# A build-time list scheduler reckons TensorE steps a tenth longer and adds a fixed wait to each step of the other compute engines

## Chip, cores and metric

One core of a Trainium2 chip runs the whole program in one launch. The metric is device microseconds of one execution, as the median of several. One further execution was taken with the hardware profiler; all durations and waits below come from it.

## What is computed

A conditioned block on x of 4 x 1024 tokens by 512 channels, all in float32: a normalised, modulated Mamba-like scan with a gated residual, then a normalised, modulated mixture of 8 experts (two per token) with another gated residual.

```python
mod = (_silu(c) @ wmod).reshape(4, 6, 1, -1)          # sa, ca, ga, sb, cb, gb
h = _layernorm(x) * (1 + ca) + sa
x = x + ga * attn(h)
h = _layernorm(x) * (1 + cb) + sb
x = x + gb * ffn(h)
...
# attn: a causal depthwise convolution of 4 taps gives u; then
x_dbl = u_bld @ xproj_w.T                              # 128 + 16 + 16 columns: dt, Bm, Cm
delta = softplus(dt @ dtproj_w.T + dtproj_b)
dA, dBu = exp(delta[..., None] * A), delta[..., None] * Bm[:, :, None, :] * u_bld[..., None]
h = dA * h + dBu                                       # over 1024 steps, 512 channels x 16 states
y = einsum('bdn,bn->bd', h, c) + u_bld * D_skip
...
# ffn: top 2 of 8 experts by tanh(x @ Wg1.T) @ Wg2.T, softmax over the two
up = einsum('td,ehd->teh', xt, Wup) + bup              # 256 hidden per expert
down = einsum('teh,eoh->teo', silu(up), Wdown) + bdown
out = einsum('te,teo->to', scores, down)
```

## The kernel before

**Tiling and stages.** The tokens are cut into nine blocks along the sequence: 512 tokens each for the first three batches (two blocks a batch), and 512, 384 and 128 for the last. Each block passes three parts. The *front* (`front`, with `conv`, `pre` and `post`) normalises, turns to channels-on-partitions, convolves, projects and makes delta and delta times u. The *recurrence* runs over 64 units a block, one for each of 16 states and 4 chunks of 128 channels. The *back* (`back`, `router`, `scatter`) normalises again, routes, and scatters rows to their experts in DRAM; then `tiles` and `expert` run 128-row tiles of one expert each, 86 in all, and `combine` gathers each token's two rows. The last block of 128 tokens goes through all eight experts in `dense` without a scatter. A branch at the end (`rest`) holds tiles for token counts that overflow; it is not entered with these inputs.

**One unit of the recurrence** goes round four engines: dB, the product of duT and a column of B, on ScalarE (L878, two instructions of 128x256 a unit in a block of 512) or as one on GpSimd (L885); its turning by TensorE into a PSUM bank pb (L919, ring of 2); da, an exponential on ScalarE (L904, ring of 4); the scan h on VectorE (L937, ring of 2 pairs); the product hc with C on GpSimd (L955, ring of 5); the sum over the states into acc on TensorE (L994). The rows of C are spread by a DMA from SyncE's queue (cq, L854, ring of 4), which waits for a ring place that hc gives back. GpSimd also copies the last column of h into `state` for the next block (L963).

**One expert tile**: SyncE loads its rows and its expert's weights (L1368, L1370: 256 KB and 1 MB; a weight ring of 4, and a fifth buffer once the fronts are done); TensorE turns the rows (px, L1395), a copy takes them out (xT, L337 on ScalarE or L339 on VectorE), TensorE multiplies (pe, L1408), VectorE adds the bias (L1419), ScalarE takes a tanh (th, L1426), VectorE multiplies (hid, L1428), TensorE multiplies again (po, L1436), VectorE scales (L1446), and SyncE stores the rows (L1449).

**What sets the order.** The tile framework is put in manual mode, so each engine's instructions stand in the order in which Python emits them. That order is made by the class `Order` while the program is built. Every part above is a generator (a thread) that yields *steps*: an engine or a choice of engines, a cost, and events to wait for. `run` repeatedly takes the step that could begin first by its own clock, and, among those of the same engine that could begin within `TOGETHER` = 0.15 us of it, the one with the smallest due time; it then lets the thread emit the instructions and sets the engine's `free` time to the step's end. What depends on it may start `HANDOFF` later (0.30, 0.17, 0.22, 0.12 us for TensorE, VectorE, ScalarE, GpSimd). Due times stand on a fixed scale of 150 us a block of 512. Costs come from small formulas; for instance

```python
def t_mm(n, times=1):
    return times * 2 * max(0.112, 0.00084 * n)
...
def t_act(n, times=1):
    return times * (0.19 + 0.00083 * n)
```

with 0.11 us for a 128x128 turn, 0.09 + 0.00104 n for VectorE, 0.09 + 0.00215 n for a scan, and 0.05 + 0.0024 n for GpSimd. Steps by `either` may go to VectorE or ScalarE (normalisation L343/L345, copies L337/L339), steps by `both` to VectorE or GpSimd (delta L772, du L775), the D-skip product to any of the three (L780/L782/L784), and dB to ScalarE or GpSimd. `begins` chooses: earliest start plus cost plus handoff, and `OTHER` = 1.0 us is added to every engine but ScalarE. Nothing of this runs on the chip: there, each engine takes its instructions in the fixed order and waits on semaphores.

Of the kernel before, what the change touches and what calls it, by code (L numbers as in the profile page):

```python
# [97 lines left out]

PE, DVE, ACT, POOL, SP = range(5)
HANDOFF = (0.30, 0.17, 0.22, 0.12, 0.0)  # L100
TOGETHER = 0.15
OTHER = 1.0
TRANSFER, KB_PER_US, KB_ALONE = 4.0, 290.0, 150.0
# [76 lines left out]
class Order:  # L180
# [19 lines left out]
    def begins(self, th):  # L200
# [8 lines left out]
        if isinstance(eng, int):  # L209
            return max(r, self.free[eng]), eng, cost  # L210
        return min(
            ((max(r, self.free[e]), e, c) for e, c in eng), key=lambda s: s[0] + s[2] + HANDOFF[s[1]] + (0.0 if s[1] == ACT else OTHER)
        )

    def run(self):
        while self.threads:
            can = [(b, th) for th in self.threads if (b := self.begins(th)) is not None]
            if not can:
                raise RuntimeError("no thread can go on: " + str([th[0].__name__ for th in self.threads]))
            t0, eng, _ = min(can, key=lambda c: c[0][0])[0]  # L220
            (t, _, cost), th = min(
                (c for c in can if c[0][1] == eng and c[0][0] <= t0 + TOGETHER), key=lambda c: c[1][3]
            )
            self.eng, kb = eng, th[1][4]
            self.start = t
            self.free[eng] = t + cost
            self.fin = t + cost + HANDOFF[eng]
            if kb:
                self.moved[eng] = max(self.moved[eng], t + cost) + kb / KB_PER_US
                self.fin = max(self.moved[eng], t + cost + kb / KB_ALONE) + TRANSFER  # L230
            th[2] = self.fin
            th[3] += th[4]
            self.advance(th)
# [1487 lines left out]
```

## Time and profile before

| what | value |
|---|---|
| median of 3 runs (lowest to highest) | 1475.49 us (1470.91 to 1481.48) |
| the profiled execution's own time | 1469.49 us |
| its span, first to last instruction | 1467.8 us |
| mean granted TensorE clock in it | 0.924 |
| instructions in it | 24446 |
| scans (L937), first and last start | 64.9 and about 1354.6 us |

The profiled execution is 6.0 us below the median and 1.4 us below the lowest of the three runs. In the tables below a row of groups reads: line, engine, operation, output and inputs, size, count, then busy us, mean ns of one, idle time of the engine just before them and what ended it. A matmul's mean includes its way through the array, so four in a row take less than four means. Stretches of the trace are named by blocks: stage k is the time in which the scans of block k run; it begins with that block's first scan (stage 1 at 185 us, 2 at 325, 3 at 475, 4 at 647, 5 at 812, 6 at 976, 7 at 1134, 8 at 1281), and what follows the last scan, from 1355 us on, is the tail.

### The profile page before, as it was taken

To read this page: it belongs to the slowest core of one execution; us is meant where nothing else is said; L and a number is where in the kernel's file an instruction comes from. 1 tells how busy PE (TensorE), PEld (TensorE's weight loads), DVE (VectorE), ACT (ScalarE), POOL (GpSimd) and SP (SyncE) were. 2 spreads that over 40 slices of the span, in tenths; PEclk is the share of its full clock that TensorE was granted. 3 is DMA by queue.
4 is the path that set the end of the run, shared out by engine and by line. 5 is a ranking of instruction groups with operands and counts; after the bars stand their busy time and mean duration, and the time that the engine had idled before them with its cause. 6 is when DMAs were issued, how large, how long until landed. Compare 5 with 4: busy or idle time off the path is not lost. (4 is left out here: it accounts for less than half of the span.)

```text
span 1467.8 us, 24446 instructions
## 1 busy us (share of the span) xinstructions
PE 1239.5 (84%) x7716; PEld 930.3 (63%) x7716; DVE 1153.6 (79%) x1870; ACT 1065.0 (73%) x2127; POOL 1029.7 (70%) x1216
## 2 busy tenths in 40 slices
PE   5588687878789889998889989989899898898686
PEld 2456555665478657775567767777687666764454
DVE  4679989899988778898887988988889889557233
ACT  2789997799689585999687686888689867456110
POOL 1478986798588466788788856888889868557202
PEclk8799998899689998999799998999899999998698
DMA  4377754757499997653688978678999976985897
GB/s 175 112 180 147 147 146 106 190 166 163 132 269 299 263 255 217 202 158 89 200 260 297 330 215 225 209 249 262 243 305 268 281 206 231 327 241 141 306 337 215
DMA packets 141933, 321.63 MB, mean 219 GB/s; under 512 B 14899, under 2 KB 43475, under 8 KB 128998
## 3 DMA queue, kind: packets, MB, share of 16 engines
q1 hardware_dynamic: 111344, 254.35, 56.4%
q0 software_dynamic: 13888, 32.58, 10.4%
q10 hardware_dynamic: 16566, 33.08, 8.7%
q8 instruction: 63, 1.03, 0.3%
q14 instruction: 72, 0.59, 0.1%
HBM read 245.95 MB, written 82.40 MB: 224 GB/s over the span
## 5 line engine op out<-in xcount | busy, mean ns | idle before, releaser
L955 POOL TENSOR_TENSOR hc<-h,cq 128x512 f32<-128x512 f32 (+2 forms) x576 | 689.1, 1283 | 191.8 <-DVE h L937 114.8
L904 ACT ACTIVATE da<-delta,a_neg 128x512 f32<-128x512 f32 (+2 forms) x576 | 380.2, 668 | 115.4 <-DVE h L937 102.4
L919 PE MATMUL pb<-ident,dB 128*128 128x128 f32 x2048 | 350.0, 294 | 81.8 <-DVE h L937 70.2
L878 ACT ACTIVATE dB<-duT,bT 128x256 f32<-128x256 f32 x856 | 381.6, 498 | 32.4 <-PE pb L919 24.5
L994 PE MATMUL acc<-ident,hc 128*128 128x128 f32 x2048 | 344.5, 292 | 64.2 <-POOL hc L955 60.8
L919 PEld LDWEIGHTS pb<-ident,dB 128*128 128x128 f32 x2048 | 252.0, 150 | 179.7 <-DVE h L937 83.0
L937 DVE TENSOR_TENSOR_SCAN h<-da,state,pb 128x512 f32<-128x512 f32 (+2 forms) x320 | 329.4, 1053 | 37.7 <-PE pb L919 15.1
L994 PEld LDWEIGHTS acc<-ident,hc 128*128 128x128 f32 x2048 | 252.6, 149 | 143.1 <-POOL hc L955 102.2
L937 DVE TENSOR_TENSOR_SCAN h<-da,pb 128x512 f32<-128x512 f32 x256 | 304.8, 1208 | 48.4 <-PE pb L919 22.5
L1408 PEld LDWEIGHTS pe<-xT,w 128*128 128x128 f32 x1376 | 172.8, 195 | 31.0 <-issue 20.5
L1408 PE MATMUL pe<-xT,w 128*128 128x128 f32 x1376 | 185.9, 280 | 4.5 <-ACT xT L337 3.9
L1436 PE MATMUL po<-w,hid 128*128 128x512 f32 x344 | 179.1, 610 | 8.2 <-DVE hid L1428 7.4
L1485 POOL DMA_INDIRECT xc<-xs,idx x56 | 90.3, 1612 | 53.2 <-DMA xc<-xs,idx 25.2
L885 POOL TENSOR_TENSOR dB<-duT,bT 128x512 f32<-128x512 f32 (+1 forms) x88 | 88.6, 1016 | 27.0 <-PE pb L919 18.5
L1446 DVE SCALAR_TENSOR_TENSOR xs<-po,xs,gbh 128x512 f32<-128x512 f32 x86 | 63.7, 740 | 38.0 <-PE po L1436 37.0
L1323 POOL DMA_INDIRECT xs<-h,idx x62 | 63.8, 1029 | 27.6 <-POOL idx L1322 12.6
L1426 ACT ACTIVATE th<-pe 128x256 f32<-128x256 f32 x86 | 32.3, 376 | 60.6 <-DVE pe L1419 60.5
L1436 PEld LDWEIGHTS po<-w,hid 128*128 128x128 f32 x344 | 54.1, 194 | 25.3 <-issue 10.6
L337 ACT COPY xT<-px 128x512 f32<-128x512 f32 x78 | 44.9, 578 | 28.2 <-PE px L1395 28.1
L1419 DVE TENSOR_TENSOR pe<-pe,w 128x256 f32<-128x256 f32 x86 | 36.2, 421 | 36.2 <-PE pe L1408 33.9
L963 POOL COPY state<-h 128x2 f32<-128x2 f32 x160 | 59.2, 370 | 0.1
L1395 PE MATMUL px<-ident,xs 128*128 128x128 f32 x344 | 53.6, 280 | 1.6 <-ACT hT L343 0.8
(200 smaller groups left out, 1536.5 us busy)
## 6 DMA issues: line engine op xcount, KB each, us to landing
w<-w_all SPq DMA_DIRECT2D x86, 1025.0 KB
cq<-scr SPq DMA_DIRECT2D x224, 256.0 KB
xs<-xs SPq DMA_DIRECT2D x86, 256.5 KB
xs<-xs SPq DMA_DIRECT2D x86, 256.0 KB
xs<-xc ACTq DMA_DIRECT2D x16, 1026.0 KB
we<-w_all SPq DMA_DIRECT2D x8, 1025.0 KB
xf<-in_x SPq DMA_DIRECT2D x32, 256.0 KB
xr<-in_x SPq DMA_DIRECT2D x14, 512.0 KB
```

Of the source, the lines that this page charges most:

```text
L878: nc.scalar.activation(dB[u // 2].t[:, t, :], duT_sb[blk][half].t[:, t, :], AF.Identity, scale=bT_sb[blk].t[:, t, n : n + 1],)
L885: engine().tensor_tensor(dB[u // 2].t[:, t0:t1, :], duT_sb[blk][half].t[:, t0:t1, :], bT_sb[blk].t[:, t0:t1, n].unsqueeze(2).to_broadcast( ...
L904: nc.scalar.activation(da[u].t[:, :ln], delta_sb[blk][half].t[:, i, :ln], AF.Exp, scale=a_neg[:, dc, n : n + 1])
L919: nc.tensor.transpose(pbs[u][:, t * P : (t + 1) * P], dB[u // 2].t[:, t, i * P : (i + 1) * P], ident)
L937: nc.vector.tensor_tensor_scan(hs[u // 2].t[:, i, :ln], da[u].t[:, :ln], pbs.pop(u)[:, :ln], 0.0 if t0 == 0 else state[:, n, dc : dc + 1], ...
L955: nc.gpsimd.tensor_tensor(hcs[u].t[:, :ln], hs[u // 2].t[:, i, :ln], cq[u // 2].t[:, :ln], ALU.mult)
L994: nc.tensor.matmul(acc[blk, dc][:, t * P : (t + 1) * P], lhsT=src.t[:, t * P : (t + 1) * P], rhs=ident, is_transpose=True, start=False, st ...
L1323: i = nc.gpsimd.indirect_dma_start(out=xs_d[g], out_offset=bass.IndirectOffsetOnAxis(ap=idx[:, k, t : t + 1], axis=0), in_=h2[k].t, in_off ...
L1408: nc.tensor.matmul(pu[:, hc * P : (hc + 1) * P], lhsT=up[:, kc, hc * P : (hc + 1) * P], rhs=xT.t[:, kc, :], start=(kc == 0), stop=(kc == D ...
L1436: nc.tensor.matmul(po, lhsT=hid.t[:, hc * P : (hc + 1) * P], rhs=w.t[:, W_DN + hc * D : W_DN + (hc + 1) * D], start=(hc == 0), stop=(hc == ...
L1446: nc.vector.scalar_tensor_tensor(xs.t[:, :D], po, xs.t[:, D:], gbh[b].t, ALU.mult, ALU.mult)
L1485: nc.gpsimd.indirect_dma_start(out=a, out_offset=None, in_=xs_d[g], in_offset=bass.IndirectOffsetOnAxis(ap=idx_sb[blk][:, choice, t : t + ...
```

## The change

Two tuples are added, and in `run` a step's cost is multiplied (by 1.1 for TensorE) and raised (by 0.06 us for VectorE, ScalarE and GpSimd) before it is entered. Steps of 0.03 us or less (waits for a ring, with no instruction) keep their cost. The cost by which `begins` chooses an engine stays as it was. No instruction is added or removed by hand, and no buffer, ring or due time changes; what changes is the order of emission and, where an engine is chosen, the choice.

```diff
 HANDOFF = (0.30, 0.17, 0.22, 0.12, 0.0)
+PACE = (1.1, 1.0, 1.0, 1.0, 1.0)
+WAIT = (0.0, 0.06, 0.06, 0.06, 0.0)
 TOGETHER = 0.15
...
             self.eng, kb = eng, th[1][4]
+            if cost > 0.03:
+                cost = cost * PACE[eng] + WAIT[eng]
             self.start = t
             self.free[eng] = t + cost
             self.fin = t + cost + HANDOFF[eng]
```

The engines stand in the order TensorE, VectorE, ScalarE, GpSimd, SyncE.

## Prediction, made before the changed kernel was run

> **What bounds the kernel now.** I read the busy totals and the TensorE clock first, then a table by stage, then the waits of the stages in which scans and expert tiles mix, then the chain that ended last.
>
> ```profile
> PE 1239.5 (84%) x7716; PEld 930.3 (63%) x7716; DVE 1153.6 (79%) x1870; ACT 1065.0 (73%) x2127; POOL 1029.7 (70%) x1216
> PEclk8799998899689998999799998999899999998698
> ```
>
> No engine is full: the kernel is four queues in fixed orders that wait for each other. By stage (span, then busy us and count of PE, PEld, DVE, ACT, POOL, then the clock, the DMA share and GB/s):
>
> ```profile
> 185.00:325.00 140.00, 110.46 (x681) 84.34 (x682) 125.91 (x183) 118.99 (x230) 113.04 (x115) 0.88 0.57 143
> 325.00:475.00 150.00, 126.93 (x798) 98.60 (x799) 130.43 (x200) 124.69 (x244) 120.16 (x148) 0.89 0.79 217
> 475.00:647.00 172.00, 152.31 (x1001) 117.02 (x1000) 142.26 (x220) 128.83 (x251) 115.31 (x115) 0.96 0.80 229
> 647.00:812.00 165.00, 141.04 (x886) 109.71 (x885) 137.46 (x214) 132.29 (x258) 134.94 (x156) 0.92 0.67 207
> 812.00:976.00 164.00, 155.01 (x1036) 120.20 (x1035) 145.73 (x229) 127.71 (x246) 122.20 (x122) 0.97 0.78 240
> ...
> 1355.00:1468.00 113.00, 79.74 (x423) 55.72 (x421) 35.87 (x84) 15.77 (x37) 24.77 (x27) 0.85 0.90 287
> ```
>
> VectorE leads in the light stages (126 of 140) and TensorE in the heavy ones (155 of 164). Over stages 1 to 8 (1170 us) the rows of this table sum to 984.5 us of VectorE and 1028.4 of TensorE: 185 and 142 us of stalls, which only the order can win or lose. Who ends them (waits in 185 to 1355 us; total, times, longest):
>
> ```profile
> DVE h L937 <- PE pb L919: 30.0, 37, 3.7
> DVE pe L1419 <- PE pe L1408: 21.0, 18, 5.5
> DVE xs L1446 <- PE po L1436: 18.1, 23, 1.7
> DVE h L937 <- POOL state L963: 12.2, 10, 2.8
> ...
> DVE h L937 <- POOL hc L955: 10.4, 9, 2.7
> ```
>
> VectorE mostly waits for TensorE. The tail is another case, the chain in order of time:
>
> ```profile
> 1373.05 0.20 POOL den L1128
> ...
> 1385.47 11.22 DMA w<-w_all
> 1396.70 14.06 DMA xs<-xs
> ...
> 1410.86 13.63 DMA we<-w_all
> ```
>
> From 1376 to 1444 us transfers set its pace, and 10 tiles and 8 dense experts of weights have to come in.
>
> **The change, part by part.** It adds no instruction: each engine's work moves in its queue or to another engine. The order in which both built programs' instructions stand shows how; lines are those of before.
>
> (a) *Costs against rows.* A 128x512 da takes 715 ns (row below), reckoned 0.615 before and 0.675 after; the bias-add L1419 takes 421, reckoned 356 and 416; hc takes 1387, reckoned 1279 and 1339. TensorE's mean clock of 0.924 means a factor of 1.08 where 1.1 is reckoned. The plan comes nearer; this alone is worth nothing on the chip.
>
> A rule speaks against the flat factor: the Trainium skill, "TensorE: Matmul & The Clock Gate", section "Part 1: The HAM clock gate", has the clock at either half or full by recent activity. The row agrees in part: L1408 matmuls last 272/275/582 ns (least, median, most), so 1.1 fits hardly any one stretch. By the row (1.08 on the mean) the plan's TensorE error shrinks from 8% to 2%; by the rule it is wrong by 10% in a fast stretch and by 45% in a slow one. I take the mean, but credit the better plan with only half its gain in (f); by the rule alone that credit is 0 and the sum 3.0 us higher.
>
> (b) *Work that changes engine.* dB: 33 fewer on ScalarE, 16 more full-size and one half-size on GpSimd. xf normalisation: 7 from ScalarE to VectorE. xT copies: 3 the same way. delta (L772): 5 full-size from VectorE to GpSimd; du (L775): 7 full-size back and two of 384 the other way. A few single copies and D-skip products move.
>
> ```profile
> L878 ACT ACTIVATE dB<-duT,bT 128x256 f32<-128x256 f32 x856 | 381.6, 498 | 32.4 <-PE pb L919 24.5 <-DMA cq<-scr 4.0 <-PE pc L1185 1.8
> L885 POOL TENSOR_TENSOR dB<-duT,bT 128x512 f32<-128x512 f32 x80 | 83.8, 1056 | 15.1 <-PE pb L919 10.4 <-ACT da L904 2.8 <-ACT duT L337 1.9
> L904 ACT ACTIVATE da<-delta,a_neg 128x512 f32<-128x512 f32 x448 | 317.5, 715 | 85.4 <-DVE h L937 73.0 <-DMA xs<-xs 5.3 <-issue 4.3
> ```
>
> VectorE, by its own rows: xf 7 x 0.974 = 6.8; du 7 x 1.314 - 2 x 1.700 = 5.8; delta -5 x 1.223 + 2 x 0.278 = -5.6; copies 3 x 0.670 + 0.67 + 0.25 - 0.5 = 2.4; pu -0.81 and D-skip -3.504 - 2 x 0.492 = -5.3 in all. Sum +4.2 us (rounding). VectorE is 84% busy in the stages (984.5 of 1170), so I charge 0.84: **+3.5**. Ends: 0 if it falls into stalls, 4.2 if not.
>
> GpSimd: dB 16 x 1.056 + 0.61 = 17.5; delta 5 x 1.318 - 2 x 0.456 = 5.7; du -7 x 1.319 + 2 x 1.003 = -7.2; D-skip about 2.2. Sum +18.2 us. Scans wait 22.6 us for GpSimd (state and hc) against its 892 us of work in the stages, 2.5%; acc waits 48.9 for hc, 5.5%. So 18.2 us costs between 0.5 and 1.0; I take **+1.0**. Its cover is a GpSimd that is at most 85% busy (135.1 of 158 us in stage 6); without that cover it costs all 18.2, since hc, the cq loads behind it on SyncE and the next scans are late.
>
> ScalarE: dB -33 x 381.6/856 = -14.7, xf -7 x 0.808 = -5.7, xT -1.7, others +0.7: -21.4. VectorE waits 44.1 us for it (da, y, th, h, xd, gbh) against its 910 us, 4.8%: **-1.0**; the end below is -21.4.
>
> (c) *The shared port.* The Trainium skill, "SBUF — State Buffer", section "Who interferes with whom", has a VectorE instruction with two SBUF inputs, or in a two-port mode, and a reading GpSimd instruction lock each other out for a whole instruction. That speaks against moving products to GpSimd and du and xf to VectorE.
>
> ```profile
> L782 DVE TENSOR_SCALAR u<-u,sm x3: 461/524/3504, 449.9 to 1245.2; 128x512 f32<-128x512 f32 x2, 128x128 f32<-128x128 f32 x1
> L775 DVE TENSOR_TENSOR du<-delta,u x16: 277/1476/3222, 55.8 to 1234.2; 128x512 f32<-128x512 f32 x11, 128x128 f32<-128x128 f32 x3, 128x384 f32<-128x384 f32 x2
> ```
>
> The longest are several times the shortest, as such a lock would make them. By the rule, 6 more such instructions (xf +7, du +5, delta -3, D-skip -3) could each wait for one hc of 1.39 us: 8 us. The row means (0.974, 1.314) already hold such waits, so I add **0**; by the rule the sum would be 8 us higher, which the range keeps.
>
> (d) *Tiles between stages.* Counted on TensorE by which block's turnings they stand among, tiles in stages 2 to 5 go from 5, 13, 7, 16.5 to 7, 11, 10, 13; stages 7, 8 and the tail keep 14, 7 and 10, and stage 6 takes half a tile more. Against stage 1 (140 us, none) stages 2 to 5 are 10, 32, 25 and 24 us longer, 2.0, 2.5, 3.6 and 1.5 a tile, 2.2 on the mean. By the mean, as many tiles come as go: **0**. By each stage's own rate, with 1.4 in stage 6: 4.0 - 5.0 + 10.8 - 5.1 + 0.7 = +5.4. Stage 4 owes its rate to its gathers as well (GpSimd 134.9), so I take the mean and keep +5.4 in the range. An evening gain would need the heavy stages to be steeper, and stage 5 is not.
>
> (e) *Start and tail.* The order up to the first scans differs in one normalisation and a copy: 0. In the tail, GpSimd now has two adding gathers (L1485) of one tile, the second waiting for the first to land, ahead of the last router's den (L1128); TensorE's turning of the scores (L1142) waits for that and stands ahead of all but the first tiles' matmuls. In the trace an add issued at 1358.98 was stored from 1364.10, some 5 us: after the last normalisation at 1365.7 the den comes between 1372.5 and 1377.5, against 1373.05: 0 to 4.5 us, take 2, largely under the queued weights. On SyncE the last out stores (L1494), which waited 9.4 us for their gathers ahead of the first dense load, now stand apart, one earlier and one behind that load. DMA share is 0.84 in 1408 to 1412 us against about 1.0 around: 0 to 4 us to win, take 2. Together **0**.
>
> (f) *Stalls.* I counted, for the 76 tiles outside the tail, where VectorE's consumer stands among the scans and TensorE's producer among the pb turnings. The bias-add stands one or two scans early in 28 tiles before and 19 after; a third of its 21.0 us is 7. For L1446 it is 19 and 21 (a tenth of 18.1, +1.9); hid stands early after its tanh in 47 and 42 (a tenth of 7.1, -0.8). Sum -5.9; half, by (a): **-3.0**. ACT's tanh waits longer, but under ScalarE's idle fifth.
>
> Sum: 3.5 + 1.0 - 1.0 + 0 + 0 + 0 - 3.0 = +0.5 us. The profiled execution took 1469.5 (its span 1467.8 and 1.7 around), so 1470.0; the median lies 6.0 higher: **1476.0 us**.
>
> **Rivals.** *The better plan removes stalls everywhere* (0.26): the pb, pe, po and pc waits of VectorE (79.8 us with pc's 10.7) fall by a quarter, not only where I counted: 20 us, 1455. For it: (a) and the later consumers. Against: pb is bound by its ring of two, not by the plan. *GpSimd becomes the bound* (0.28), the other side: the 18.2 us no longer hide, from the point at which a stage's GpSimd work nears its span. Stage 4 has 134.9 of 165 and gains three dB; stages 1 and 2 have 113.0 of 140 and 120.2 of 150 and gain four each. Then 18.2 on the path with little back: 1494. Against: hc still waits 99.3 us for h in these stages, so GpSimd is mostly early. *The change does nothing that shows* is my forecast (0.46): all orders moved, equal and opposite gains.
>
> **How the numbers follow.** This kernel's measurement tells about 1% from no change: 1460.7 to 1490.2. The first rival lies below, the second above, mine within, so faster 0.26, same 0.46, slower 0.28. My own case runs from -10 to +14 (part of the ends of b to f at once): 1466 to 1490. The range reaches to both rivals with 4 or 5 us beyond: 1450 to 1498.
>
> **What would show it.** Right: VectorE busy near 1158, GpSimd near 1048, ScalarE near 1044 us; fewer waits of L1419 for L1408; stages 3 and 5 some 5 to 8 us shorter, 2 and 4 longer by as much; a tail within 4 us of 113. Wrong: scans waiting for hc or state more than twice 22.6 us, den in the tail late by over 5 us, or VectorE's stalls in the stages off 185 by more than 15 us either way.

## The result and the profile after

The changed kernel took 1488.69 us (median of 20 runs, 1479.13 to 1495.29) against 1472.78 of the kernel before (20 runs, 1467.75 to 1487.93): a ratio of 1.0101 [1.0083, 1.0119]. Forecast was no measurable change (1476.0); it is about 1% slower, on the border of what was called telling. The profiled execution after has a span of 1488.1 us, 20.3 more than the one before.

The page of the kernel after, busy totals (the mean granted TensorE clock is 0.913, before 0.924):

```profile
PE 1245.9 (84%) x7716; PEld 934.1 (63%) x7716; DVE 1164.6 (78%) x1879; ACT 1047.8 (70%) x2084; POOL 1046.8 (70%) x1234
```

Work went from ScalarE to GpSimd as forecast (1044 and 1048 were named); VectorE came to 1164.6, not 1158. No engine became full. By stage (columns as in the prediction; stages 1 to 6, then the tail):

```profile
193.00:332.00 139.00, 110.08 (x678) 85.07 (x677) 127.36 (x185) 115.30 (x222) 116.66 (x116) 0.88 0.54 144
332.00:485.00 153.00, 130.82 (x835) 102.77 (x836) 133.18 (x206) 121.51 (x236) 121.72 (x151) 0.89 0.80 218
485.00:644.00 159.00, 143.82 (x955) 110.56 (x954) 142.29 (x218) 122.88 (x237) 116.92 (x118) 0.97 0.87 240
644.00:812.00 168.00, 142.11 (x909) 109.30 (x908) 143.54 (x219) 126.83 (x246) 140.83 (x160) 0.93 0.70 211
812.00:972.00 160.00, 149.67 (x1007) 115.97 (x1006) 143.23 (x223) 125.84 (x242) 121.42 (x123) 0.98 0.77 238
972.00:1145.00 173.00, 149.85 (x986) 118.33 (x984) 141.01 (x218) 133.34 (x274) 136.06 (x156) 0.94 0.89 252
...
1364.00:1488.00 124.00, 81.97 (x424) 57.05 (x423) 35.61 (x84) 16.00 (x37) 27.74 (x31) 0.82 0.85 262
```

To a tenth, by the scans' starts, the lengths before and after are:

| | start | s0 | s1 | s2 | s3 | s4 | s5 | s6 | s7 | s8 | tail |
|---|---|---|---|---|---|---|---|---|---|---|---|
| before | 64.9 | 120.3 | 140.0 | 150.0 | 171.5 | 164.8 | 164.3 | 157.8 | 147.5 | 73.9 | 112.8 |
| after | 67.6 | 125.3 | 139.0 | 152.7 | 159.0 | 168.1 | 160.6 | 172.9 | 145.6 | 72.8 | 124.5 |

Stages 1 to 8 together grew by 0.9 us, where +0.5 was forecast, but only because 15.1 us lost in stage 6 meet 14.2 won in the others. The 20 us come from the start and stage 0 (+7.7) and the tail (+11.7), and stage 6 eats what stages 3 and 5 won. Stage 6 of the kernel before, for comparison:

```profile
976.00:1134.00 158.00, 145.30 (x973) 114.14 (x972) 135.00 (x216) 128.56 (x265) 135.09 (x155) 0.96 0.95 272
```

VectorE has 6.0 us more work in this stage, TensorE 4.6 and GpSimd 1.0; the rest of the 15 us is waiting. Who ends VectorE's waits in stages 1 to 8 of the kernel after:

```profile
DVE h L941 <- PE pb L923: 35.4, 46, 2.8
DVE xs L1450 <- PE po L1440: 30.1, 29, 4.3
DVE h L941 <- POOL state L967: 26.8, 11, 5.4
DVE pe L1423 <- PE pe L1412: 11.3, 14, 2.1
```

The bias-add's wait fell from 21.0 to 11.3 us, as forecast; the scans' wait for `state` rose from 12.2 to 26.8 and the scaling's for po from 18.1 to 30.1. `state` is a copy of 0.2 us (median) on GpSimd, so something ahead of it in that queue may stand still.

**What stands still on GpSimd.** `combine` issues two adding gathers a tile (L1489); the second, into the same rows, waits for the first to land, and GpSimd's queue waits with it. Stage 6 of the kernel before, these gathers alone (durations, then what ended the idle time before them: us, times):

```profile
L1485 POOL DMA_INDIRECT xc<-xs,idx x18: 1552/1598/1709, 975.1 to 1131.8; - x18
  DMA xc<-xs,idx: 3.2, 1
```

The same of the kernel after, where the landings of this stage take 5.1 / 8.6 / 11.7 us from issue (least, median, most):

```profile
L1489 POOL DMA_INDIRECT xc<-xs,idx x19: 1555/1599/1704, 973.0 to 1142.2; - x19
  DMA xc<-xs,idx: 15.9, 5
```

One of the five in GpSimd's own timeline (start, length, idle time before and its releaser): the first gather at 1095.26, 5.6 us of other work behind it (hc, `state`, a dB), then 3.76 us of nothing until it has landed; the next hc starts at 1106.66.

```profile
1095.26 1.58 POOL L1489 DMA_INDIRECT xc<-xs,idx  x1 [0.16 <-issue]
...
1105.63 1.60 POOL L1489 DMA_INDIRECT xc<-xs,idx  x1 [3.76 <-DMA xc<-xs,idx]
```

A likely reason lies in the plan. It lets the second gather begin when the first one's transfer should be done, some 7 us after its start by the kernel's own formula (a fixed 4.0 us, 1.6 us of issue and 256 KB at its rate); measured landings over the whole execution of the kernel after are 4.9 / 8.1 / 11.7 us. The change makes compute steps longer in the plan but leaves transfers as they were. So the plan now fits less real work of GpSimd between the two gathers: by the durations of the kernel before, a median of 5.8 us instead of 6.3, and 21 pairs of 28 have under 6.5 us, before 15.

**The tail.** The chain that ended last, kernel after:

```profile
1421.68 15.13 DMA we<-w_all
1436.94 2.96 PE pue L1544 x16
...
1441.48 1.78 PE pe L1412 x16
...
1454.63 0.87 PE po L1440 x2
1455.53 0.75 DVE xs L1450
1456.31 8.26 DMA xs<-xs
```

TensorE has the last tile's pe and po behind the first dense expert's matmuls (pue), which wait for weights until 1436.94. The tile's scaling begins on VectorE 92 us after the last scan, before 73; its store lands 8.26 us later, and only then can the last gathers start.

### The profile page after: what moved, and what is told of

It is laid out like the page before. It is cut to its first block, busy times and chain, and to the rows that moved or that the text cites. A ratio compares the mean times of both kernels' runs of the same rounds, so it can differ in the third digit from the quotient of the medians.

```text
span 1488.1 us, 24436 instructions
## 1 busy us (share of the span) xinstructions
PE 1245.9 (84%) x7716; PEld 934.1 (63%) x7716; DVE 1164.6 (78%) x1879; ACT 1047.8 (70%) x2084; POOL 1046.8 (70%) x1234
## 5 line engine op out<-in xcount | busy, mean ns | idle before, releaser
L882 ACT ACTIVATE dB<-duT,bT 128x256 f32<-128x256 f32 x823 | 368.5, 499 | 52.8 <-PE pb L923 44.3
L1489 POOL DMA_INDIRECT xc<-xs,idx x56 | 90.6, 1618 | 80.6 <-DMA xc<-xs,idx 41.9
L889 POOL TENSOR_TENSOR dB<-duT,bT 128x512 f32<-128x512 f32 (+1 forms) x105 | 108.1, 1059 | 35.4 <-PE pb L923 25.8
L1327 POOL DMA_INDIRECT xs<-h,idx x62 | 63.9, 1031 | 34.2 <-POOL idx L1326 13.5
L1440 PEld LDWEIGHTS po<-w,hid 128*128 128x128 f32 x344 | 54.5, 195 | 24.2 <-issue 10.4
L1399 PE MATMUL px<-ident,xs 128*128 128x128 f32 x344 | 55.3, 287 | 2.3 <-DMA xs<-xs 2.0
L967 POOL COPY state<-h 128x2 f32<-128x2 f32 x160 | 54.7, 342 | 0.1
```

What stands on the lines that cost most here:

```text
L882: nc.scalar.activation(dB[u // 2].t[:, t, :], duT_sb[blk][half].t[:, t, :], AF.Identity, scale=bT_sb[blk].t[:, t, n : n + 1],)
L889: engine().tensor_tensor(dB[u // 2].t[:, t0:t1, :], duT_sb[blk][half].t[:, t0:t1, :], bT_sb[blk].t[:, t0:t1, n].unsqueeze(2).to_broadcast( ...
L1327: i = nc.gpsimd.indirect_dma_start(out=xs_d[g], out_offset=bass.IndirectOffsetOnAxis(ap=idx[:, k, t : t + 1], axis=0), in_=h2[k].t, in_off ...
L1440: nc.tensor.matmul(po, lhsT=hid.t[:, hc * P : (hc + 1) * P], rhs=w.t[:, W_DN + hc * D : W_DN + (hc + 1) * D], start=(hc == 0), stop=(hc == ...
L1489: nc.gpsimd.indirect_dma_start(out=a, out_offset=None, in_=xs_d[g], in_offset=bass.IndirectOffsetOnAxis(ap=idx_sb[blk][:, choice, t : t + ...
```

## The experiments

Ratios are to the kernel before on the same chip, so kernels are compared by ratio, not by their us; the changed kernel itself was measured on one chip only, and how far ratios from different chips can be compared is said at the end of this section. Four theories were to be told apart. *Gathers*: GpSimd stands between a tile's two adding gathers because the plan times their landing too short. *Load*: GpSimd's extra 17 us of work are the cost, the second rival of the prediction. *TensorE's order* in the tail: the last tile waits behind the dense matmuls. *Store*: its last store waits behind dense loads on SyncE. The expectations divide them otherwise: "queue theory" there is any instruction that holds up what stands behind it in its queue (so gathers, TensorE's order and the store together), "load theory" is the second of the four, and "lottery theory" is a fifth, that many small shifts of order add up with no one cause.

### The last store ahead of the dense loads (e_store, on the kernel after)

```diff
-            yield step(SP, 0.5, ring("w", 4), laid, mine, after=[], kb=1024)
+            put = [event("put")] if e >= 4 else []
+            yield step(SP, 0.5, ring("w", 4), laid, mine, after=put, kb=1024)
```

with `event("put")` set in `expert` by the last row store of the last group.

> The changed kernel with one row store moved: the last expert tile's store (behind four dense weight loads on SyncE in the changed kernel) goes ahead of them; all else keeps its order. Queue theory (instructions that hold up a queue cost the time): the tail loses the 8 to 10 us between the fourth-last dense load and that store, so 1479 us, 1.004 of before. Load theory (GpSimd's 17 us of added work cost it) and lottery theory (many small reshuffles): no change, 1488 us, 1.010.

Measured: 1494.67 us, ratio 1.0083 [1.0053, 1.0113]; the tail took 128.3 us, 3.8 more. In the kernel after, SyncE issued four dense loads from 1445.02 on and the last store at 1456.31. Its queue in this one:

```profile
1444.78 14.34 SPq L1453 DMA_DIRECT2D xs<-xs  x2
1459.21 2.14 SPq L1539 DMA_DIRECT2D we<-w_all  x4
```

The store waits all the same, since VectorE hands the rows over late, and now holds four weight loads behind it. The store theory falls: being behind the loads was not what delayed the store.

### TensorE's part of the last tile ahead of the dense experts (e_tail, on the kernel after)

```diff
+        if g == NG - 1 and j == n_main(g) - 1:
+            event("lastpe").t = o.start
...
-            yield step(PE, t_mm(n, HC * DC), banks, *h2_in)
+            yield step(PE, t_mm(n, HC * DC), banks, *h2_in, *([event("lastpe")] if e == 0 else []))
```

> The changed kernel with TensorE's work of the last expert tile put ahead of the first dense expert's, which waits for its weights from DRAM; until then the order is the same. Queue theory: the last tile no longer waits behind that load, the tail falls from 124 to about 117 us, 1.005 of before. Load and lottery theory: 1.010.

Measured: 1476.64 us, ratio 1.0058 [1.0038, 1.0079]; the tail took 117.5 us instead of 124.5. TensorE's timeline:

```profile
1440.69 1.05 PE L1412 MATMUL pe<-xT,w 128*128 128x128 f32 x8
1445.79 3.40 PE L1546 MATMUL pue<-h2T,we 128*128 128x128 f32 x16 [4.05 <-DMA we<-w_all]
```

The last tile's pe now stands before the time in which pue waits for its weights, and its po follow at 1449.03 (before the edit, the last at 1454.47). So some 7 us of the tail are this order on TensorE, and the ratio fell by 0.4%, as that would make it; the other 4.7 us by which the tail is longer than before stay.

### A later landing in the plan (e_gap, on the kernel after; e_gapb, on the kernel before)

```diff
+        landed = Event()
+        landed.t = 0.0
         for choice in range(2):
-            yield step(POOL, 1.6, x1_in, event("stored", g), kb=256)
+            yield step(POOL, 1.6, x1_in, event("stored", g), landed, kb=256)
+            landed.t = o.fin + 3.0
```

> The changed kernel with the second adding gather of each row tile planned 3 us later after the first; work between the two on GpSimd is then 8.6 us in the median by the rows, where the changed kernel has 5.8 and before 6.3. Queue theory: GpSimd's idle time that ends with a landed gather falls from 41.9 us to under 15, stage 6 (173 us) goes back to about 160, the late store in the tail stays; 1472 to 1482 us. Load theory: 97 products dB on GpSimd, half way between 88 and 105, so about 1480 us with the idle time at no account. Lottery: anything from 1465 to 1495.

> The kernel before with the second adding gather planned 3 us later, as was done to the changed kernel (0.989 of before there). If the new costs are worth something once the gathers are out of the way, this one gains less: 0.995. If the gap is all there is to it, it comes to 0.989 as well. Lottery: anything from 0.985 to 1.015.

Measured: on the kernel after 1466.22 us, ratio 0.9886 [0.9856, 0.9915]; on the kernel before 1458.6 us, 0.9933 [0.9909, 0.9958]. One number in the plan takes the changed kernel from 1.0% slower to 1.1% faster, with stage 6 at 159.5 us. Stage 6 of e_gap, the gathers:

```profile
L1492 POOL DMA_INDIRECT xc<-xs,idx x18: 1585/1606/1732, 974.0 to 1130.6; - x18
  DMA xc<-x1d: 2.9, 2
...
  DMA xc<-xs,idx: 0.4, 1
```

GpSimd's work in e_gap is 1040.7 us, still 11.0 more than before; load as the cost does not fit that. But the plan reorders all engines when one of its numbers moves, so these two alone do not prove that the gathers did it. Nor was the gain forecast: the waits alone should have brought a ratio of 1.000 to 1.006, so some of it is something else.

### The second gather later on GpSimd, all else as it stood (e_defer, on the kernel after; e_deferb, on the kernel before)

```diff
+            if choice and g + 1 < NG:
+                held_back.append([2, add])
+                mine = held_back[-1]
+            else:
+                add()
```

`add` issues the gather; it comes after two more hc, or at the latest ahead of the rows' out store. TensorE, VectorE and ScalarE keep their orders.

> The changed kernel with one thing moved: the second adding gather of each row tile stands up to two hc products later in GpSimd's queue (8.6 us of work between the two in the median, was 5.8); TensorE, VectorE and ScalarE keep their order, and GpSimd keeps its 105 products dB. Queue theory (the early second gather holds up GpSimd, and with it scans): idle time ended by a landed gather from 41.9 us to under 15, stage 6 back to about 160 us, 1.000 to 1.004 of before. Load theory and lottery theory: nothing but gathers moved, so 1.010 stays.

> The same deferral in the kernel before (9.4 us of work between, was 6.3). Queue theory: less to win, since its gathers held up GpSimd for 25.2 us and mostly in the tail, 0.993 to 0.998. Load and lottery theory: 1.000.

Measured: e_deferb 1461.43 us, ratio 0.9951 [0.9929, 0.9972]; e_defer 1481.36, 1.0103 [1.0062, 1.0144]. On the kernel before the forecast held: GpSimd's idle time ahead of these gathers fell from 31.8 to 12.5 us in stages 4 to 8, and these stages from 708.3 to 702.9 us. On the kernel after it failed: stage 6 stayed at 171.2 us. Its gathers there:

```profile
L1497 POOL DMA_INDIRECT xc<-xs,idx x18: 1567/1596/1693, 968.9 to 1134.6; - x18
  DMA out<-xc: 8.6, 1
  DMA xc<-x1d: 5.9, 1
...
  DMA xc<-xs,idx: 1.8, 1
```

The wait of gather for gather is gone (15.9 to 1.8), but the next tile's *first* gather now waits for the out store of the tile that held its buffer (8.6) and for its rows (5.9). There are two xc buffers; whoever comes later in one keeps the other waiting. GpSimd's idle time ahead of gathers in stage 6 goes from 21.1 to only 19.1. So the wait moved, and this run cannot say what stage 6 would take without it. A third buffer wasn't tried.

### The first gather later, all else as it stood (e_earlyb, on the kernel before)

The same edit with `if not choice`: the first gather of a tile comes up to two hc later and so nearer to the second (median of the work between them 3.0 us).

> The kernel before with the first adding gather of each row tile moved up to two hc products later in GpSimd's queue, so that 3.0 us of work stand between the two in the median instead of 6.3; the other engines keep their order and GpSimd its 88 products dB. Queue theory (a gather that waits holds up GpSimd and with it the scans): GpSimd's idle time before gathers in stages 4 to 8 goes from 32 us to 60 or more, stage 6 from 158 us to 168 or more, 1.008 to 1.020 of before. Load and lottery theory: 1.000.

Measured: 1547.2 us, ratio 1.0426 [1.0389, 1.0463]. The waits of the whole execution:

```profile
POOL xc L1493 <- DMA xc<-xs,idx: 91.3, 18, 12.0
...
DVE h L937 <- POOL state L968: 54.6, 12, 8.5
```

This run tells most. The same line of the kernel before:

```profile
POOL xc L1485 <- DMA xc<-xs,idx: 25.2, 8, 6.5
```

With every other engine's order and every engine's work kept, gathers nearer together make GpSimd stand 91.3 us for landings (before 25.2, after 41.9), and the scans then wait 54.6 us for `state`, just what the kernel after showed in a smaller dose. Stages 4 to 8 go from 708.3 to 784.9 us for 55.3 us more of idle time ahead of gathers: more than that time itself. TensorE's mean clock fell from 0.924 to 0.896, and its 7716 matmuls were busy for 1271.5 us instead of 1239.5; how much of the time that cost, no run separates. The forecast (1.008 to 1.020) had the direction and too small a size.

### Each half of the change alone (e_wait, e_pace)

e_wait sets `PACE = (1.0, 1.0, 1.0, 1.0, 1.0)`, e_pace sets `WAIT = (0.0, 0.0, 0.0, 0.0, 0.0)`.

> Only the 0.06 us a step, TensorE at its old cost. 104 products on GpSimd, gathers as close as in the changed kernel (22 of 28 pairs under 6.5 us of work between), the last store behind three dense loads and ahead of the fourth. Queue theory: as slow as the changed kernel but for part of the tail, 1480 to 1488 us. Load theory: 1488 us. Lottery: anything from 1465 to 1495.

> Only TensorE's factor of 1.1, no added wait. 93 products on GpSimd, gathers as in before (16 of 28 pairs under 6.5 us), the last store behind four dense loads. Queue theory: before plus 8 us of tail, 1478 to 1483 us. Load theory: five of 17 products, 1477 us. Lottery: anything from 1465 to 1495.

Measured: e_wait 1504.6 us, ratio 1.0149 [1.0109, 1.0188]; e_pace 1499.34, 1.0113 [1.0080, 1.0145]. Either half alone is as bad as both, so the two do not add up, and both are slower than any theory but the lottery forecast. e_pace speaks against load: GpSimd's work is 1034.8 us, only 5.1 more than before, and it is as slow as the kernel after. It speaks as much against the count of work between two gathers: 16 of 28 pairs have under 6.5 us, about as before (15), and over the whole execution GpSimd stands for landings just as long as before:

```profile
  DMA xc<-xs,idx: 25.2, 9
```

In its stage 6 only half of the 20.9 us ahead of gathers are landings (10.4); 4.8 are for the gather's own rows and 3.6 for the tiles' row stores. The scans wait 16.0 us for `state` there all the same. Stage 6 takes 169.9 us in e_wait and 172.8 in e_pace, and stage 4, at 173.0 and 178.7 (before 164.8), is long as well; the cause of that stays open.

### A weight load at its old place (e_wm, on the kernel after)

In stage 0 the sixth piece of the modulation weights (1 MB) is loaded from ScalarE's queue when a given scan of the plan is done. In the kernel before it is issued at 83.08 us, 13.2 after the fifth piece. In the kernel after it is issued at 78.10. ScalarE's timeline there, 14 us later:

```profile
91.92 0.91 ACT L882 ACTIVATE dB<-duT,bT 128x256 f32<-128x256 f32 x2 [6.99 <-DMA cq<-scr]
```

It follows the fifth piece by 5.5 us, and the small cq loads that the scans need come late: hc waits 5.2 us for one (before none) and dB 7.0 (before 4.0).

```diff
-            yield step(ACT, 0.35, ring("w", 4), event("h", 2 + 4 * (s - 3)), kb=1024)
+            yield step(ACT, 0.35, ring("w", 4), event("h", 2 + 4 * (s - 3) + (4 if s == 5 else 0)), kb=1024)
```

> The changed kernel with the sixth piece of the modulation weights (1 MB, by ScalarE's queue) loaded after 18 instead of 12 exponentials. If that load holds up the spread of C in stage 0 (5.2 us at hc and 7.0 at dB there, against 0 and 4.0 before), stage 0 falls from 125 to about 120 us; what comes after is ordered anew and not forecast: 1.000 to 1.012.

Measured: 1489.68 us, ratio 1.0048 [1.0029, 1.0067]; stage 0 took 121.7 us instead of 125.3. That fits, with a reserve. The wait of dB for cq is gone, but hc still waits 4.8 us. Five kernels have stage 0 in the order of the kernel before, with 120.3 to 123.4 us; five have it in that of the kernel after, with 122.9 to 126.2; the two with the load moved have 121.7 and, in e_best, 119.6. So the load is worth some 3 us of stage 0, little more than one profile differs from the next. The order after stage 0 changed here too, so the rest of the ratio's fall (0.5% in all, some 8 us) is not shown to be the load's.

### The repairs together (e_gapbtail, on the kernel before; e_best, on the kernel after)

e_gapbtail is the later landing and the last tile ahead; e_best is these two and the load at its old place.

> The kernel before with both cures: the second gather planned 3 us later, and the last tile's TensorE work ahead of the first dense expert. Its last tile stood ahead already, so the tail gains nothing: 0.990 to 0.995, as with the gap alone. It is the measure for the next kernel.

> The changed kernel with the gap (0.989 of before by itself), with the last tile's TensorE work first (worth 0.004) and with the sixth piece of the modulation weights loaded six units later. If the three are separate: 0.980 to 0.985. If the gap's gain was luck of one order: anything from 0.985 to 1.010.

Measured: e_gapbtail 1463.96 us, ratio 0.9869 [0.9833, 0.9904]; e_best 1457.61 us (1453.98 to 1461.9), 0.9824 [0.9789, 0.9859]: faster than both kernels, by 1.8% and some 2.7%.

**All profiles side by side.** GpSimd's idle time ahead of adding gathers, whatever ended it, in stage 6 and in stages 4 to 8; the part of it in stage 6 that a landed gather ended; and the lengths of stage 6 and the tail. Each row is one profile; those of e_tail and e_wm, not in the table, come from executions 13 and 12 us above their medians.

| kernel | ratio | idle in s6 | of it landings | idle in s4 to s8 | stage 6 | tail |
|---|---|---|---|---|---|---|
| before | 1 | 8.2 | 3.2 | 31.8 | 157.8 | 112.8 |
| e_gapb | 0.9933 | 6.7 | 1.5 | 15.8 | 156.9 | 111.0 |
| e_gapbtail | 0.9869 | 6.7 | 0.3 | 17.2 | 156.5 | 112.3 |
| e_deferb | 0.9951 | 4.5 | 0.7 | 12.5 | 157.3 | 112.2 |
| e_earlyb | 1.0426 | 27.1 | 20.7 | 87.1 | 186.4 | 118.4 |
| after | 1.0101 | 21.1 | 15.9 | 44.7 | 172.9 | 124.5 |
| e_defer | 1.0103 | 19.1 | 1.8 | 30.2 | 171.2 | 125.4 |
| e_gap | 0.9886 | 10.3 | 0.4 | 18.5 | 159.5 | 129.7 |
| e_best | 0.9824 | 13.5 | 1.3 | 22.4 | 164.2 | 124.3 |
| e_wait | 1.0149 | 15.0 | 7.9 | 35.7 | 169.9 | 116.9 |
| e_pace | 1.0113 | 20.9 | 10.4 | 46.5 | 172.8 | 124.1 |

Stage 6 takes 156.5 to 159.5 us with at most 10.3 us of this idle time and 168.6 to 172.9 with 15 to 22.4 (e_store, e_tail and e_wm lie there too); e_best stands between, at 13.5 and 164.2. Landings alone do not order the rows: e_wait has 7.9 us of them, its scans wait 2.6 us for `state`, and stage 6 is long for other reasons; e_best has 1.3, with 8.3 us of waiting for the gathers' own rows. TensorE's clock in this stage is 0.99 in e_gap and 0.93 in e_best; what set it, no run shows.

**How far a ratio carries.** e_gapbtail has the orders of e_gapb on every engine up to the last expert tile, and its tail is 1.3 us longer in the profile. Yet its ratio is 0.9869 [0.9833, 0.9904] against 0.9933 [0.9909, 0.9958], measured on another chip. So 0.6% between ratios from two chips is no finding by itself. Above that stand e_earlyb, and e_gap against e_store, e_wait and e_pace, which were measured on one chip (0.9886 against 1.0083 to 1.0149).

**What is shown and what is not.** Shown, with the other engines' orders and all the work kept: gathers nearer together cost time (e_earlyb). Farther apart they won 0.5% on the kernel before (e_deferb): little, and measured on one chip, though stages 4 to 8 shortened with it. Shown by the profiles: TensorE's order costs 7 us of the tail. Shown: GpSimd's load alone is not the cost, since e_gap and e_best carry 11.0 and 11.6 us more of it than the kernel before and are faster. Not proved: that all 15 us of stage 6 are the gathers'. The one run that moved them alone there (e_defer) met the next wait, the runs that freed stage 6 reordered everything, and in e_wait and e_pace stage 6 is as long with fewer landings to wait for (7.9 and 10.4 us against 15.9). So the lottery theory stands as a part of the cost: without e_earlyb, orders of nearly the same work lie between 0.982 and 1.015. Open: the start, 2.7 us longer, 4.7 us of the tail, and whether the new costs are worth anything of themselves. With the later landing in both, the changed costs lead by 0.5% (0.9886 against 0.9933), as they do with the tail mended too (0.9824 against 0.9869, e_best having the load as well), but the intervals overlap.

## Why the prediction was off, step by step

The time lies inside the stated range (1450 to 1498) and by a hair inside the prediction's own case (1466 to 1490). Much of that is luck. The forecast sum for stages 1 to 8 (+0.5, measured +0.9) came out because stage 6 lost what the other stages won, and neither was in the sum at its size; the range was that wide for two rivals. The 20.3 us between the two profiles are, all but 0.9, where the sum had 0: in (e).

**Busy times (b): right for two engines, off for the third.** ScalarE 1047.8 (1044 forecast) and GpSimd 1046.8 (1048). VectorE rose by 11.0 us where its own rows gave 4.2.

**The shared port (c): the rule of the Trainium skill came nearer.** By the rows this term was 0, by "SBUF — State Buffer", section "Who interferes with whom", +8. Two groups of VectorE in the kernel after (count, busy us, mean ns):

```profile
L779 DVE TENSOR_TENSOR du<-delta,u 128x512 f32<-128x512 f32 x18 | 25.9, 1440 | 1.1 <-POOL delta L776 1.1
...
L776 DVE TENSOR_TENSOR delta<-delta,y 128x384 f32<-128x384 f32 x4 | 9.8, 2442 | 0.0
```

The same four deltas took 823 ns each before; the two 128-column deltas at 278 ns became four at 1275; du rose from 1314 to 1440. Against these, three du of 128 columns fell from 1979 to 321. The four come to 7.8 us, about the 6.8 by which VectorE's 11.0 exceed the forecast 4.2. The failed step is "the row means already hold such waits": a mean held the overlaps of the order in which it was taken, not those of the new one. No run forced the overlap, so that it is the lock is the rule's reading.

**Scans waiting for GpSimd (b, second part): this failed.** The prediction charged GpSimd's extra work at a share of past waits and took 1.0 us. The waits for `state` and hc went from 22.6 us to 31.3 (4.5 of them for hc), under the twofold that was named as the sign, but 8.7 more is well over 1.0. The cause, as far as e_earlyb and e_gap show it, was another: not load, but GpSimd standing at the second of two gathers. The prediction saw that pair once, in the tail (e), with "some 5 us" to land read from one transfer; landings in the kernel after are 8.1 us at the median and 11.7 at most. It never asked how often such a pair stands in the kernel: 28 times.

**Tiles between stages (d): right in sign, not in the sum.** Stage 3 got shorter by 12.5 us, more than the 5 to 8 named, and 5 by 3.7, less; 2 and 4 grew by 2.7 and 3.3. Stages 2 to 5 together won 10.2 us, where the mean rate gave 0 and the stages' own rates 4.7 lost. Stage 6 with "half a tile more" was reckoned at +0.7 and grew by 15.1, far beyond what a tile cost anywhere (1.5 to 3.6).

**Start and tail (e): failed, and it is the main miss: 19.4 us where 0 stood.** The den came 4.7 us later after the last scan (22.75 against 18.05), just past the end of the range of 0 to 4.5. As forecast, it stands behind a gather that waits for its partner (GpSimd idle 4.71 us until 1385.35, den at 1386.35). But that was not the main price. The last tile's TensorE work stands behind the first dense expert's, which the prediction did not look at; e_tail shows 7.0 of the tail's 11.7 us for it, against a forecast of 0 within 4. The first tile's rows are also loaded 3.7 us later (16.7 us after the last scan instead of 12.9), with other gathers ahead of the last scatters; what that cost is not separated, nor whether SyncE's stores won their 2. The start, forecast as 0, cost 2.7, and its cause stays open. Stage 0, also held to be untouched, cost 5.0; e_wm gives some 3 of it to an early weight load that the prediction did not look for.

**Stalls (f): the counted parts came half true.** VectorE's stalls in stages 1 to 8 went from 185.5 to 175.7, within the 15 us named; the 9.8 won there (3.0 forecast) meet 10.8 us more work of VectorE in these stages (3.5 charged). The bias-add gained 9.7 us (7 forecast); the scaling lost 12.0 (1.9 forecast): counting places in the order told the sign for both, and the size for one.

**The rivals.** "The better plan removes stalls" had 20 us of them go in the stages; 9.8 went, and the time did not fall. "GpSimd becomes the bound" named nearly the right time (1494), but load is not the reason: e_pace adds 5.1 us of GpSimd's work and is as slow, e_gap adds 11.0 and is faster.

## What to carry to other kernels

An order made at build depends on how its costs stand to each other: compute and transfers are best measured together. Here, 10% and 0.06 us more for the compute steps alone gave a slower order, and 3 us more for one transfer a faster one in both kernels. Before costs are changed, list every pair in which an instruction waits, in an engine's own queue, for a transfer issued by the same engine, and see how much real work stands between them against the longest measured landing. One changed cost reorders everything, so a theory of it is tested by moving the one instruction with all other orders kept (e_deferb, e_earlyb). In any reordering, look at the tail and at the small loads of the first stage apart: a stage's work can be the same and its order still put a ready tile behind one that waits for weights.

## What the runs showed of the hardware

The adding gathers of 256 KB took 4.9 / 8.1 / 11.7 us from issue to landing (least, median, most) in the kernel after, so one number for it in a plan is short for many of them unless it lies near the top. And a queue that stands can take more than its own time: in e_earlyb, 55.3 us more of idle time on GpSimd went with 76.6 us more in five stages, and with a mean granted TensorE clock of 0.896 over the execution instead of 0.924.
